# Softplus of a 16-state scan as one ScalarE function in place of a composition

## The chip, the cores and the metric

The kernel runs on one core of a Trainium2 chip. The metric is the device time of one execution in microseconds (us); lower is better. Everything is in 32-bit floating point.

## The reference, cut to what matters

The whole computation is a two-layer network on four images of 128 channels and 64x64 pixels. Layer 0 reorders the pixels of each image by a score, runs a selective scan with 16 states over the 4096 reordered pixels, and puts the result back. Layer 1 runs a scan with 256 states and then a long convolution. The change lies in layer 0's scan:

```python
xc = silu(conv1d(xm) + conv1d_b)                   # 256 channels, 4096 tokens
dbc = xc @ x_proj_w.T                              # 8 + 16 + 16 columns
dt_low, Bc, Cc = dbc[..., :8], dbc[..., 8:24], dbc[..., 24:]
dt = softplus(dt_low @ dt_proj_w.T + dt_proj_b)    # dt_proj_b is -4.6
dA = exp(dt[..., None] * A)                        # A = -exp(A_log), 16 states
dBx = dt[..., None] * Bc[:, :, None, :] * xc[..., None]
h = dA_t * h + dBx_t                               # one step of the scan
y = einsum('bds,bs->bd', h, C_t) + D * xc
y = y * silu(z)
```

So softplus, log(1 + exp(x)), is taken once for every channel and token, 4 x 256 x 4096 values in all.

## The kernel before, in words

The program runs in three parts: a front (layer 0 up to the reordered pixels), `layer0_scan`, and layer 1. The order of the instructions on each engine in `layer0_scan` is written out by hand: engines work through their own list in that order and wait for each other by semaphores.

*Units and steps.* `layer0_scan` cuts each image's 4096 tokens into 8 units of 512 tokens (`PJ`), 32 units in all. A unit has 16 steps: two halves of 256 tokens (`SUB`), times 8 pairs of states. The 256 channels are two halves (`k`) of 128 partitions. Each step works on 128 x 1024 values: two states, two halves of channels, 256 tokens.

*One step.* Every engine has a part in it:

- `fetch` (SP) broadcasts the rows of Bc and Cc for two states to all partitions, five steps ahead, into `bcb` (six buffers).
- `spread` (POOL, L549) multiplies `dx` by the Bc rows into `v` (four buffers), three steps ahead. A small second instruction (L554) adds the state carried over from the half before; `carry` (L544) prepares this from `af`.
- `lift` (ScalarE, L563) computes the factors exp(dt * A) with four Exp activations of 128 x 255 into one of two PSUM buffers `factors`, one step ahead.
- `scan` (VectorE) runs the recurrence (L571) into `states`, then the product with the Cc rows (L575) and a small copy (L576).
- `add_up` (TensorE, L587) sums the products over the states in PSUM; at the end of each half `gated` (VectorE, L603) multiplies the sum by silu(z) into `yg`.

*Beside the steps.* The generator `project` prepares the inputs of the next unit while the present one is scanned. `beside`, called once a step, takes pieces from it. Each `yield` names the kind of the piece that follows: "free" pieces are issued one per step; "mm" and "post" pieces are a matmul into the single PSUM buffer `mm` and what empties it in the next step. `project` yields, in order: two convolutions by four matmuls each (L410, emptied by L415 into `xz`), two matmuls for z (L419, L421), Silu in place on `xz` (L423), the projection to Bc, Cc and dt_low (L427, L430), two matmuls for dt (L439), softplus, the product `dx` of dt and xc (L458, POOL), and `af`, the factors of each half's first token (L463). For unit 0 the whole of `project` is issued before the first step, and unit 1's begins directly behind it.

*Softplus.* It is composed as relu(x) + log(1 + e) + (e - ((1 + e) - 1)), with e = exp(-|x|); the last term gives back what rounding 1 + e loses. Abs (L441) and Relu (L442) read the matmul's PSUM buffer, Exp (L444) runs in place, and Identity with a bias of one (L447), Ln (L449) and Identity with a bias of minus one (L450) follow in one piece; then come three POOL instructions (L452, L454, L456), one to a piece. All but Abs and Relu are 128 x 1024.

*Other side work.* `output` multiplies `yg` by the output weights (L479, copied out by ScalarE at L483) and, once for each of the first three images, `put_back` returns the pixels to their places (L499, VectorE at L505, with `xs` loaded from DRAM). They share the buffer `mm` with `project`, which goes first.

*Tables.* ScalarE's functions come from tables, of which one set is active at a time; the compiler puts a table load (ACT_TABLE_LOAD) before an activation whose function is not in the active set.

The main loop sets the order within a step:

```python
    for j in range(-9, steps):
        if 0 <= j + 5 < steps:
            bcs[j + 5] = fetch(j + 5)
        ...
            vs[j + 3] = spread(j + 3, bcs[j + 3])
        if 0 <= j + 1 < steps:
            lift(j + 1)
        ...
        prods[j] = scan(j, vs.pop(j), bcs.pop(j))
        if j:
            add_up(j - 1, prods.pop(j - 1))
        beside(j)
```

Of the kernel before, what the change touches and what calls it, by code (L numbers as in the profile page):

```python
# [8 lines left out]
F32 = mybir.dt.float32  # L9
AF = mybir.ActivationFunctionType  # L10
ALU = mybir.AluOpType
# [322 lines left out]
PJ = 512  # L334
# [3 lines left out]
def layer0_scan(ctx: ExitStack, tc, ident, w, x, xnt, permd, x2, omd, psum, following):  # L338
# [7 lines left out]
    nc = tc.nc  # L346
    ctx.enter_context(tc.manual_schedule())
    cp = ctx.enter_context(tc.tile_pool(name="b_c", bufs=1))
    big = ctx.enter_context(tc.tile_pool(name="b_big", bufs=2))
    sm = ctx.enter_context(tc.tile_pool(name="b_sm", bufs=1))  # L350
# [10 lines left out]
    def halves(name, src):  # L361
        return load(name, [128, 2], src.rearrange("(k p) -> p k", p=128))
# [9 lines left out]
    db = halves("db", w["dt_proj_b"])  # L372
# [6 lines left out]
    nc.vector.tensor_scalar(an, an, -1.0, None, ALU.mult)  # L379
    ow = load("ow", [128, 2, 128], w["out_proj_w"].rearrange("(k p) c -> p k c", p=128))  # L380
    last = cp.tile([128, NS, 2], F32, name="last")
    one, minus = (cp.tile([128, 1], F32, name=name) for name in ("one", "minus"))
    nc.vector.memset(one, 1.0)
    nc.vector.memset(minus, -1.0)
    factors = [pa.tile([128, 2, 2, SUB], F32, name=f"f{i}") for i in range(2)]
    for da in factors:
        nc.vector.memset(da[:, :, :, 0:1], 0.0)  # L387
# [2 lines left out]
    def middle():  # L390
        return ps_.tile([128, 512], F32, tag="mm", name="mm")
# [5 lines left out]
    def project(b, unit, into):  # L397


        xz, dt, dx, af, bcd = into  # L400
        xin = big.tile([128, 3 + PJ], F32, tag="xin", name="xin")
        nc.sync.dma_start(xin, xnt[b][:, bass.ds(PJ * unit, 3 + PJ)])
        yield "free"
        yield "free"
        for k in range(2):
            yield "mm"
            ps = middle()
            for i in range(4):

                nc.tensor.matmul(  # L410
                    ps, taps[:, i, bass.ts(k, 128)], xin[:, bass.ds(i, PJ)], start=i == 0, stop=i == 3
                )
            yield "hold"
            yield "post"
            nc.scalar.activation(xz[:, k, :], ps, AF.Identity, bias=cb[:, k : k + 1])  # L415
        for k in range(2):
            yield "mm"
            ps = middle()
            nc.tensor.matmul(ps, win[:, bass.ts(2 + k, 128)], xin[:, 3:], start=True, stop=True)  # L419
            yield "post"  # L420
            nc.scalar.copy(xz[:, 2 + k, :], ps)  # L421
        yield "free"
        nc.scalar.activation(xz, xz, AF.Silu)  # L423
        yield "mm"
        ps = middle()
        for k in range(2):
            nc.tensor.matmul(ps[:96], xw[:, k, :], xz[:, k, :], start=k == 0, stop=k == 1)  # L427
        yield "post"
        bc = big.tile([96, PJ], F32, tag="bc", name="bc")
        nc.scalar.copy(bc, ps[:96])  # L430
        nc.sync.dma_start(bcd[0], bc[32 : 32 + NS, :])
        nc.sync.dma_start(bcd[1], bc[64 : 64 + NS, :])


        e = sm.tile([128, 2, PJ], F32, tag="e", name="e")
        for k in range(2):
            yield "mm"
            ps = middle()
            nc.tensor.matmul(ps, dw[:, bass.ts(k, 128)], bc[0:8, :], start=True, stop=True)  # L439
            yield "post"  # L440
            nc.scalar.activation(e[:, k, :], ps, AF.Abs, bias=db[:, k : k + 1])  # L441
            nc.scalar.activation(dt[:, k, :], ps, AF.Relu, bias=db[:, k : k + 1])  # L442
        yield "free"
        nc.scalar.activation(e, e, AF.Exp, scale=-1.0)  # L444
        yield "free"
        e1 = sm.tile([128, 2, PJ], F32, tag="e1", name="e1")
        nc.scalar.activation(e1, e, AF.Identity, bias=one)  # L447
        ln = sm.tile([128, 2, PJ], F32, tag="ln", name="ln")
        nc.scalar.activation(ln, e1, AF.Ln)  # L449
        nc.scalar.activation(e1, e1, AF.Identity, bias=minus)  # L450
        yield "free"
        nc.gpsimd.tensor_tensor(e, e, e1, ALU.subtract)  # L452
        yield "free"
        nc.gpsimd.tensor_tensor(dt, dt, ln, ALU.add)  # L454
        yield "free"
        nc.gpsimd.tensor_tensor(dt, dt, e, ALU.add)  # L456
        yield "free"
        nc.gpsimd.tensor_tensor(dx, dt, xz[:, 0:2, :], ALU.mult)  # L458
        yield "free"
        yield "free"  # L460
        for i in range(PJ // SUB):
            for k in range(2):
                nc.scalar.activation(  # L463
                    af[:, i, :, k], an[:, k, :], AF.Exp, scale=dt[:, k, SUB * i : SUB * i + 1]
                )
# [153 lines left out]
    for _ in project(*units[0], ready[0]):  # L619
        pass  # L620
# [3 lines left out]
    def beside(j):  # L624
        nonlocal rear, holder
        if holder:
            keep = holder.kind == "hold"
            holder.next()
            holder = holder if keep else None
        if ahead[0] < len(units) and j >= per * (ahead[0] - 1) - 9:  # L630
            ready[ahead[0]] = tiles()
            fronts.append(Work(project(*units[ahead[0]], ready[ahead[0]])))
            ahead[0] += 1
        if j == steps - 64:
            extra.append(Work(following))
        while fronts and fronts[0].kind is None:
            fronts.pop(0)
        if (rear is None or rear.kind is None) and behind:
            rear = Work(behind.pop(0))
        for work in (*fronts, rear, *extra):  # L640
            if work and work.kind == "free":
                work.next()
        for work in (*fronts, rear, *extra):
            if work and work.kind == "mm" and holder is None:
                work.next()
                holder = work
# [768 lines left out]
@with_exitstack  # L1415
def conv_attn_hybrid(ctx: ExitStack, tc, w, out):
    nc = tc.nc
    const = ctx.enter_context(tc.tile_pool(name="const", bufs=1))
    dram = ctx.enter_context(tc.tile_pool(name="dram", bufs=1, space=DRAM))
    ident = const.tile([128, 128], F32, name="ident")  # L1420
    make_identity(nc, ident)
    half = const.tile([128, 32], F32, name="half")
    nc.vector.memset(half, -0.5)
    x2 = dram.tile([NB, 128, L], F32, name="x2")
    x3 = dram.tile([NB, 128, L], F32, name="x3")
    x = w["x"]
    xnt = dram.tile([NB, 128, 3 + L], F32, name="xnt")
    pqd = dram.tile([NK, 2, 128, 4, 128], F32, name="pqd")
    mud = dram.tile([128, 4, 3, 128], F32, name="mud")
    permd = dram.tile([128, NB, 2, 256], F32, name="permd")  # L1430
    omd = dram.tile([2, 128, 16, 128], F32, name="omd")
    layer0_front(tc, ident, half, w, x, xnt, permd, pqd, mud)
    pool = ctx.enter_context(tc.tile_pool(name="weights", bufs=1))
    weights = layer1_weights(nc, pool, *(w[k] for k in ("W_in", "W_delta", "W_B", "W_C", "W_out", "A")))
    psum, second = [], []
    work = projection(ctx, tc, ident, half, weights, x2, psum, second)
    first = work[-2](0)
    layer0_scan(tc, ident, w, x, xnt, permd, x2, omd, psum, work[-1](0, 0, first))
    layer1(tc, ident, weights, work, psum, second, w["phi"], pqd, mud, x, omd, permd, first, x2, x3, out)
# [48 lines left out]
```

## Time and profile before

| what | value |
|---|---|
| median of 3 runs | 21374.23 us |
| lowest and highest run | 21372.89 and 21374.53 us |
| profiled execution, first to last instruction | 21377.5 us |
| scan of layer 0, start of first to start of last scan instruction | 626.4 to 2735.4 us |
| VectorE busy, whole span | 20559.4 us (96%) |
| POOL busy, whole span | 20113.6 us (94%) |
| ScalarE busy, whole span | 16041.0 us (75%) |
| TensorE busy, whole span | 17653.8 us (83%) |

The profile comes from one execution, and its span is 3.3 us longer than the median of the runs. In its rows the engines are PE (TensorE matmul), PEld (TensorE weight load), DVE (VectorE), ACT (ScalarE), POOL (GpSimd) and SP (which issues the DMAs). L571 is line 571 of the kernel before. A row of the costliest groups has the line, engine and operation, output <- inputs by name, shapes and count, then the busy time in us and the mean of one instruction in ns, then the engine's idle time just before those instructions and what ended most of it. A row of a timeline has the start and the duration in us; x4 joins four like instructions, and a bracket gives the idle time before and what ended it. A row of a wait view has the total in us, the number of waits and the longest.

### The profile page before, as it was taken

What the parts mean: (1) busy time and instruction counts of PE and PEld (TensorE: products, weight loads), DVE (VectorE), ACT (ScalarE), POOL (GpSimd) and SP (SyncE); (2) the same over time, 40 slices, a digit from 0 to 9 for tenths busy, and PEclk for the clock granted to TensorE, in tenths of its full rate; (3) what the DMA queues carried; (4) which work ended last, traced back from release to release, by engine and by line L of the source; (5) the groups of instructions that cost most, each with busy time, mean ns of one, the idle gap of its engine ahead of it and who ended that gap; (6) DMA issues with size and microseconds to landing.
All of it is one profiled execution on the core that took longest, in us unless ns stands there. A gap on an engine that the chain in (4) does not pass through costs nothing.

```text
span 21377.5 us, 294496 instructions
## 1 busy us (share of the span) xinstructions
PE 17653.8 (83%) x99308; PEld 7751.4 (36%) x99308; DVE 20559.4 (96%) x11871; ACT 16041.0 (75%) x29620; POOL 20113.6 (94%) x5685
## 2 busy tenths in 40 slices
PE   7788854555858888877868999599999999999997
PEld 4344421222323333342323344243434434334434
DVE  7788899999999999999999999999999999999996
ACT  3677767777777777777777777787887787788875
POOL 2677789999999999999999999999999999999996
PEclk8999965776979999998979999799999999999999
DMA  1455554555757777766656777577777777777776
GB/s 68 127 140 139 142 161 153 179 175 167 219 172 221 220 225 222 219 211 194 208 183 220 229 236 237 172 235 232 238 232 229 233 234 233 233 233 230 231 231 189
DMA packets 2499932, 4304.08 MB, mean 201 GB/s; under 512 B 803400, under 2 KB 1322864, under 8 KB 2495216
## 3 DMA queue, kind: packets, MB, share of 16 engines
q1 hardware_dynamic: 2498416, 4285.24, 65.6%
q8 instruction: 784, 12.85, 0.2%
q14 instruction: 732, 6.00, 0.1%
HBM read 3660.02 MB, written 624.17 MB: 200 GB/s over the span
## 4 chain that ended last, share of the span: by engine, by line
DVE 51%; PE 12%; POOL 8%; issue 7%; ACT 6%; DMA 2%; SPq 0%; DVEq 0%; POOLq 0%; ACTq 0%
DVE s L1261 50%; POOL v L1238 8%; PE conv L1195 7%; ACT da L1258 5%; PE yp L1278 3%; PE fin L1137 1%; DMA dlb<-delta 1%; DMA strip<-in_phi 1%; DMA yd<-ye 0%; DVE v L1250 0%; ACT ye L1284 0%; PE mm L1052 0%; ACT t L820 0%; PE mm L884 0%; DVE st L805 0%
## 5 line engine op out<-in xcount | busy, mean ns | idle before, releaser
L1238 POOL TENSOR_TENSOR v<-u,dlb 128x2044 f32<-128x2044 f32 (+1 forms) x4096 | 18223.6, 4518 | 66.2 <-DMA dlb<-delta 42.9
L1261 DVE TENSOR_TENSOR_SCAN s<-da,v 128x1024 f32<-128x1024 f32 x8192 | 18008.3, 2286 | 187.8 <-ACT da L1258 132.0
L1258 ACT ACTIVATE da<-dlb,at 128x511 f32<-128x511 f32 x16384 | 11303.8, 690 | 1984.6 <-DVE s L1261 1485.0
L1195 PE MATMUL conv<-strip,tok 128*128 128x512 f32 (+3 forms) x20480 | 8643.5, 549 | 60.4 <-DMA strip<-in_phi 60.1
L1278 PE MATMUL yp<-s,c 128*32 128x256 f32 x65536 | 4948.7, 431 | 2610.8 <-DVE s L1261 1129.6
L1195 PEld LDWEIGHTS conv<-strip,tok 128*128 128x128 f32 x20480 | 3661.2, 191 | 4152.0 <-issue 3704.2
L1278 PEld LDWEIGHTS yp<-s,c 128*32 128x32 f32 x65536 | 1963.6, 120 | 6385.9 <-issue 2055.4
L1242 ACT COPY v<-vf 128x4 f32<-128x4 f32 x4096 | 814.6, 199 | 2121.4 <-DVE s L1261 2105.0
L1137 PE MATMUL fin<-conved,pq 128*128 128x512 f32 (+1 forms) x3968 | 1786.6, 543 | 10.4 <-ACT sum L1158 5.3
L549 POOL TENSOR_TENSOR v<-dx,bcb 128x1024 f32<-128x1024 f32 x512 | 1207.3, 2358 | 437.5 <-DVE states L571 431.5
L571 DVE TENSOR_TENSOR_SCAN states<-f,v 128x1024 f32<-128x1024 f32 x512 | 1175.9, 2297 | 173.8 <-ACT f L563 125.6
L563 ACT ACTIVATE f<-dt,an 128x255 f32<-128x255 f32 x2048 | 973.5, 476 | 399.2 <-DVE states L571 348.4
L1284 ACT COPY ye<-yp 128x512 f32<-128x512 f32 x2048 | 1186.1, 579 | 26.1 <-PE yp L1278 25.4
L1207 ACT COPY conved<-conv 128x512 f32<-128x512 f32 (+1 forms) x1728 | 986.8, 571 | 224.7 <-PE conv L1195 222.7
L587 PE MATMUL y<-p,ident 128*128 128x512 f32 x2048 | 1008.9, 621 | 132.7 <-DVE p L575 129.1
L1137 PEld LDWEIGHTS fin<-conved,pq 128*128 128x128 f32 x3968 | 662.5, 192 | 383.4 <-issue 283.7
L575 DVE TENSOR_TENSOR p<-states,bcb 128x1024 f32<-128x1024 f32 x512 | 627.1, 1225 | 38.6 <-DVE states L571 0.9
L587 PEld LDWEIGHTS y<-p,ident 128*128 128x128 f32 x2048 | 370.8, 196 | 663.4 <-issue 360.1
L479 PE MATMUL mm<-ow,yg 128*32 128x128 f32 x2048 | 281.2, 296 | 106.5 <-ACT om L483 105.3
L479 PEld LDWEIGHTS mm<-ow,yg 128*32 128x32 f32 x2048 | 235.4, 138 | 212.7 <-ACT om L483 128.4
L410 PE MATMUL mm<-xin,taps 128*128 128x512 f32 x512 | 237.8, 608 | 34.3 <-DVE f L387 20.3
L452 POOL TENSOR_TENSOR e<-e,e 128x1024 f32<-128x1024 f32 x32 | 75.1, 2346 | 197.7 <-DMA bcb<-bcd 162.0
(241 smaller groups left out, 5971.7 us busy)
## 6 DMA issues: line engine op xcount, KB each, us to landing
dlb<-delta SPq DMA_DIRECT2D x4096, 512.0 KB, 4.2
strip<-in_phi SPq DMA_DIRECT2D x1536, 448.0 KB, 4.8
yd<-ye SPq DMA_DIRECT2D x2048, 256.0 KB, 4.1
strip<-in_phi SPq DMA_DIRECT2D x1088, 256.0 KB, 4.4
bcb<-bcd SPq DMA_DIRECT2D x1024, 256.0 KB, 4.2
pq<-pqd SPq DMA_DIRECT2D x1472, 64.0 KB, 3.7
yt<-yd SPq DMA_DIRECT2D x4096, 4.0 KB, 3.4
pq<-pqd SPq DMA_DIRECT2D x256, 128.0 KB, 4.0
```

Of the source, the lines that this page charges most:

```text
L549: nc.gpsimd.tensor_tensor(v, ready[n][2][:, :, bass.ts(i, SUB)].unsqueeze(1).broadcast_to((128, 2, 2, SUB)), bc[:, 0].unsqueeze(2).broadca ...
L563: nc.scalar.activation(factors[j % 2][:, a, k, 1:], ready[n][1][:, k, SUB * i + 1 : SUB * i + SUB], AF.Exp, scale=an[:, k, 2 * g + a : 2 * ...
L571: nc.vector.tensor_tensor_scan(states.rearrange(flat), factors[j % 2].rearrange(flat), v.rearrange(flat), 0.0, ALU.mult, ALU.add)
L587: nc.tensor.matmul(t.rearrange("p k t -> p (k t)"), ident, p[:, a].rearrange("p k t -> p (k t)"), start=g == 0 and a == 0, stop=False, ski ...
L1137: nc.tensor.matmul(fin[:, bass.ds(c0, w)], pq[:, n, :], u[:, bass.ds(c0, w)], start=begin and n == 0, stop=end and not partly, skip_group_ ...
L1195: nc.tensor.matmul(ps[:, skip:], tok[:, 1 - r if side else r, j, :], strip[:, bass.ds(c0 - lo, TS - skip)], start=which == 0 and j == js[0 ...
L1207: nc.scalar.copy(u[:, cols], ps[:, cols])
L1238: nc.gpsimd.tensor_tensor(v[:, 0:n, :, 1:], ready[0][:, :, 1:].unsqueeze(1).broadcast_to((128, n, 2, TS - 1)), dl[:, 0:n, 1:].unsqueeze(2) ...
L1258: nc.scalar.activation(da[:, h, 1:], dl[:, d % VD, 1:], AF.Exp, scale=at[:, h, d : d + 1])
L1261: nc.vector.tensor_tensor_scan(s[:, d % GD].rearrange("p h t -> p (h t)"), da.rearrange("p h t -> p (h t)"), v[:, d % VD].rearrange("p h t ...
L1278: nc.tensor.matmul(yp[i // 2][bass.ts(q, 32), i % 2], c[:, h, t], s[:, :, h, t], start=h == 0, stop=h == 1)
L1284: nc.scalar.copy(ye, yp[j].rearrange("p i d t -> p i t d"))
```

## The change

Softplus is taken by ScalarE's function of that name. The matmul's PSUM buffer is emptied into `dt` by one Identity activation per half with the bias, and one Softplus activation of 128 x 1024 follows in place. Abs, Relu, Exp, the two Identity activations with constants, Ln and the three POOL instructions go, with their tiles `e`, `e1` and `ln`, the constants `one` and `minus` and four of the pauses (`yield "free"`) between the pieces.

```diff
-    one, minus = (cp.tile([128, 1], F32, name=name) for name in ("one", "minus"))
-    nc.vector.memset(one, 1.0)
-    nc.vector.memset(minus, -1.0)
...
-        e = sm.tile([128, 2, PJ], F32, tag="e", name="e")
         for k in range(2):
             yield "mm"
             ps = middle()
             nc.tensor.matmul(ps, dw[:, bass.ts(k, 128)], bc[0:8, :], start=True, stop=True)
             yield "post"
-            nc.scalar.activation(e[:, k, :], ps, AF.Abs, bias=db[:, k : k + 1])
-            nc.scalar.activation(dt[:, k, :], ps, AF.Relu, bias=db[:, k : k + 1])
+            nc.scalar.activation(dt[:, k, :], ps, AF.Identity, bias=db[:, k : k + 1])
         yield "free"
-        nc.scalar.activation(e, e, AF.Exp, scale=-1.0)
-        yield "free"
-        e1 = sm.tile([128, 2, PJ], F32, tag="e1", name="e1")
-        nc.scalar.activation(e1, e, AF.Identity, bias=one)
-        ln = sm.tile([128, 2, PJ], F32, tag="ln", name="ln")
-        nc.scalar.activation(ln, e1, AF.Ln)
-        nc.scalar.activation(e1, e1, AF.Identity, bias=minus)
-        yield "free"
-        nc.gpsimd.tensor_tensor(e, e, e1, ALU.subtract)
-        yield "free"
-        nc.gpsimd.tensor_tensor(dt, dt, ln, ALU.add)
-        yield "free"
-        nc.gpsimd.tensor_tensor(dt, dt, e, ALU.add)
+        nc.scalar.activation(dt, dt, AF.Softplus)
         yield "free"
         nc.gpsimd.tensor_tensor(dx, dt, xz[:, 0:2, :], ALU.mult)
```

## The prediction

> **What bounds the kernel now.** I began with the costliest groups of the page, to find the stage that the change touches and its engine.
>
> ```profile
> span 21377.5 us, 294496 instructions
> ...
> L549 POOL TENSOR_TENSOR v<-dx,bcb 128x1024 f32<-128x1024 f32 x512 | 1207.3, 2358 | 437.5 <-DVE states L571 431.5
> L571 DVE TENSOR_TENSOR_SCAN states<-f,v 128x1024 f32<-128x1024 f32 x512 | 1175.9, 2297 | 173.8 <-ACT f L563 125.6
> L563 ACT ACTIVATE f<-dt,an 128x255 f32<-128x255 f32 x2048 | 973.5, 476 | 399.2 <-DVE states L571 348.4
> ```
>
> The last columns say who waits. POOL's products waited 431.5 us for VectorE's scans, ScalarE's factors 348.4 us: both are fed by VectorE. In the other direction VectorE waited 125.6 us for ScalarE. By its line's own answer, the scan runs from 626.4 to 2737.7 us: 512 steps in which VectorE spends 2.30 (scan) + 1.23 (product p) + 0.15 (copy) us and, with the gaps, 3.81 us a step. So this stage is bound by VectorE, and only its waits can be won. The wait view of VectorE for 626 to 2740 us lists them (total, times, longest):
>
> ```profile
> DVE states L571 <- ACT f L563: 125.6, 61, 61.0
> DVE yg L603 <- PE y L593: 46.5, 38, 2.2
> DVE xs L505 <- DMA xs<-in_x: 22.8, 6, 7.1
> ```
>
> One of the 61 waits is the start (61.04 us before the first scan). The other 60 are 64.5 us: picked out of VectorE's timeline, 28 are 1.7 us or longer (58.2 us: mostly 2.10 or 1.87, the first 3.75) and 32 are under 0.5 us (6.3 us). To see what makes the long ones I read one unit of 16 steps, first ScalarE's timeline (start, duration), then VectorE's.
>
> ```profile
> 1618.35 2.00 ACT L563 ACTIVATE f<-dt,an 128x255 f32<-128x255 f32 x4
> 1620.41 0.69 ACT L441 ACTIVATE e<-mm,db 128x512 f32<-128x512 f32 x1
> 1621.00 0.68 ACT L442 ACTIVATE dt<-mm,db 128x512 f32<-128x512 f32 x1
> 1621.57 1.05 ACT L444 ACTIVATE e<-e 128x1024 f32<-128x1024 f32 x1
> 1622.51 2.01 ACT L563 ACTIVATE f<-dt,an 128x255 f32<-128x255 f32 x4
> ...
> 1625.15 1.15 ACT L447 ACTIVATE e<-e,one 128x1024 f32<-128x1024 f32 x1
> 1626.32 1.28 ACT L449 ACT_TABLE_LOAD   x1
> 1627.61 1.06 ACT L449 ACTIVATE ln<-e 128x1024 f32<-128x1024 f32 x1
> 1628.70 1.15 ACT L450 ACTIVATE e<-e,minus 128x1024 f32<-128x1024 f32 x1
> 1629.87 1.28 ACT L563 ACT_TABLE_LOAD   x1
> 1631.16 2.00 ACT L563 ACTIVATE f<-dt,an 128x255 f32<-128x255 f32 x4
> ```
>
> ```profile
> 1627.48 2.30 DVE L571 TENSOR_TENSOR_SCAN states<-f,v 128x1024 f32<-128x1024 f32 x1
> ...
> 1633.26 2.30 DVE L571 TENSOR_TENSOR_SCAN states<-f,v 128x1024 f32<-128x1024 f32 x1 [2.10 <-ACT f L563]
> ```
>
> Between two sets of factors ScalarE does 6.6 us of other work (1624.52 to 1631.16). Two factor buffers allow it one set ahead, so the next scan, free at 1631.2, starts 2.1 us late. The short waits come the same way from Silu (table, Silu, table: 4.5 us). In the three units per kernel in which the put-back runs, VectorE waits for the DMA of xs instead (7.1 us at most), and there is no long wait on ScalarE.
>
> **What the Trainium skill says.** "ScalarE: Activation LUTs", section "What ACT_TABLE_LOAD costs": a load is 1283 ns and about 1380 ns of drain come with it; every function runs one element a cycle, and with immediate scale and bias costs 186 ns + 0.833 ns an element, 1039 ns for 1024. The trace agrees on the load (1283 ns) and the rate (Exp 1055, Ln 1057 ns), but shows no drain: Ln starts 0.01 us after its load, the load 0.02 us after the work before it. Section "Table sets: the hidden batching unit": a load is needed at each change of set, and Exp and Ln share one. Here they don't: Ln has a load before it and Exp one after it in each unit. "TensorE: Matmul & The Clock Gate", section "Part 1: The HAM clock gate": half clock after an idle window of about 3.4 us. The trace has both: eight taps matmuls take 5.93 us after a long idle time and 3.70 us when they follow closely.
>
> **The change part by part.** The compiled order of the changed program is the old one on TensorE and SP, waits included, and on VectorE but for the two lost memsets (0.06 us each); only ScalarE's and POOL's change.
>
> 1. *Abs goes, Relu becomes Identity.* 64 Activates of 0.68 us go. One remains per half, and the next factors start 0.57 us earlier.
> 2. *Exp, the two additions of a constant and Ln go; one Softplus comes.* Per unit 1.055 + 1.145 + 1.148 us go, and Softplus takes Ln's place. No Softplus is in the trace. I take 1.06 us, as Exp and Ln; from below 1.04 by the skill's page, from above Silu's rate, (1.911 us for 2048), which gives the same. The loads stay: Softplus has one before it, the factors one after it, 62 in the loop as before. One goes at the start.
> 3. *Three POOL instructions of 2.35 us go per unit* (225.6 us). POOL waits for VectorE's scans, so this is nothing, except at the start. A gain for VectorE through less traffic I put at nothing: its product takes 1224 to 1227 ns whatever POOL does. If POOL were late, its longest wait of some 2.4 us would end first; its load only falls.
> 4. *Four pauses go*, so af and dx come up to four steps earlier. af's 0.9 us fits into the 1.2 us that ScalarE has left in a step with a copy of om (3.81 - 2.01 - 0.58); dx's 2.35 us is twice POOL's 1.1 us of waiting in a step, and the four v buffers, three steps ahead, cover it as they cover four such instructions now.
>
> *ScalarE in a unit.* The factors at 1618.35 move to 1617.78, ending 1619.8. Identity waits for its matmul as Abs did: 1620.41 to 1621.10. Load to 1622.40, Softplus to 1623.48, load to 1624.78, factors to 1626.80. The scan that they feed is due at 1627.48: 0.7 us spare. Then om's copy (0.58) and the next factors to 1629.4, due at 1631.2. The long wait is gone, and nothing replaces it. In the units with the longer matmul wait everything shifts together (Abs at 1686.24, scan at 1693.30): again 0.7. In the first unit of the loop the pattern is tighter: Abs waits for a slow matmul; I get factors at 638.8 for a scan due at 637.7, a wait of 1.1 in place of 3.75. Gain: 58.2 - 1.1 = **57 us**. Late next: VectorE itself, the Silu waits (6.3 us) and yg's wait for TensorE.
>
> *The start* (unit 0 runs bare, and unit 1's matmuls before the first scan):
>
> ```profile
> 607.62 0.91 ACT L463 ACTIVATE af<-an,dt 128x16 f32<-128x16 f32 x4 [5.91 <-POOL dt L456]
> 608.43 0.66 ACT L415 ACTIVATE xz<-mm,cb 128x512 f32<-128x512 f32 x1
> ...
> 626.41 2.30 DVE L571 TENSOR_TENSOR_SCAN states<-f,v 128x1024 f32<-128x1024 f32 x1 [61.04 <-ACT f L563]
> ```
>
> af needs dt, so it waits for POOL, and xz of unit 1 stands behind it on ScalarE, and with it TensorE, Silu and the first factors. After: second Identity to 592.1, load, Softplus to 594.5, load, af to 596.7; unit 1's matmuls, 1.2 us earlier, end at 597.8. So xz starts there instead of 608.43: 10.6 us. The next eight matmuls (6.30 us after 10 us idle) follow after 0.8 us and should take 3.70: 2.6 more. POOL has dx near 597 and the first v well before the scan at 613. Gain **13 us** (10.6 if they stay slow).
>
> *Sum:* 57 + 13 = 70 us, at the profiled span: 21377.5 to 21307.5. The views show no time around the span; it is 3.3 us above the median of the runs, 21374.2, so I forecast **21304 us**. The second layer starts after the last output copy of this stage and its program is the same; the gain is carried to the end.
>
> **The rivals.**
> *TensorE's clock moves yg's wait.* After Silu, yg waits 0.73 us where the xw matmuls are quick (18 times) and about 2.2 where they are slow (12 times: 3.63 against 1.96 us). The unit gets shorter and TensorE loses its 3.92 us idle stretch, so this may fall either way: all slow costs 18 x 1.47 = 26 us (gain 44, 21330 us), all quick gives 18 more (88, 21286). With a slow start of 2.6 us too it ends within the bound, 21333.
> *The wait only moves.* If 1 us of unseen time lies at Softplus (a drain), 0.3 us of wait is left in 28 units: gain 60, 21314. With the page's 1.38 us drain at both loads it is 2.1 us, 58 us in all: 12 to 13 left, 21362, no change. The trace's loads without drain speak against it.
> *Slower: Softplus isn't a one-element-a-cycle function.* Place: the same two loads and Softplus. It decides from about 4.2 us a call, since 1.06 + 0.7 spare + the 2.1 us of the old wait + the start's share is used up. At an eighth of the rate, 7.0 us, the wait is 5.2 us in 28 units, 147 against 58, the start gives 7: 21456 us. Silu, Gelu, Exp and Ln all run at one rate, which speaks against.
> *It doesn't do what it says* if Softplus were expanded into several instructions; the compiled order shows one Activate and one load.
>
> **How the numbers follow.** About 0.2% (43 us) is what a measurement can tell from no change. Forecast, with the clock's play: 0.87, of which 0.02 falls within the bound. The wait moves: 0.08, 0.05 of it within. Slow Softplus: 0.04. Rest 0.01 within. Faster 0.88, within 0.08, slower 0.04. Range 21281 (all quick, and 5 us more) to 21334 (all slow and a slow start).
>
> **What would show it.** Right: Softplus near 1.06 us x32; the idle time of VectorE at L571's line on ScalarE down from 125.6 to about 56 (48 at the start, 6 from Silu, 1); first scan near 613 us; period of a plain unit from 64.4 to 62.3 us; POOL's busy time down 226 us and ScalarE's 152, without use beyond this. Wrong: Softplus over 1.8 us, a gap beside its loads, long waits left on the factors, yg's waits well off 46 us, or a longer second layer.

## The result, and the profile after

| kernel | median of 7 runs, us | lowest to highest |
|---|---|---|
| before | 21374.53 | 21372.89 to 21383.01 |
| changed | 21320.29 | 21311.79 to 21323.59 |

The ratio is 0.9973 with a 95% interval of 0.9962 to 0.9984: 54 us, a quarter of a per cent, faster. The forecast was 21304 us, 70 us faster, with a range of 21281 to 21334 us. The range held; of the 70 us, 54 came. Repeated beside the experiments on another occasion the changed kernel gave 21317.41 against 21375.78 us, 58 us.

The page of the changed kernel (same columns as before; lines have moved up by 17, so L554 is the scan, L546 the factors, L532 POOL's products):

```profile
span 21321.9 us, 294235 instructions
...
L532 POOL TENSOR_TENSOR v<-dx,bcb 128x1024 f32<-128x1024 f32 x512 | 1208.0, 2360 | 631.4 <-DVE states L554 625.3
...
L546 ACT ACTIVATE f<-dt,an 128x255 f32<-128x255 f32 x2048 | 977.7, 478 | 489.6 <-DVE states L554 438.5
L554 DVE TENSOR_TENSOR_SCAN states<-f,v 128x1024 f32<-128x1024 f32 x512 | 1176.0, 2297 | 105.5 <-ACT f L546 53.8
```

VectorE's wait for the factors fell from 125.6 to 53.8 us. The two engines that feed it wait longer for it than before: POOL 625.3 instead of 431.5 us, which is what most of the time of the three lost POOL instructions per unit turned into, and ScalarE 438.5 instead of 348.4 us. VectorE's wait view for 590 to 2690 us (total, times, longest):

```profile
DVE yg L586 <- PE y L576: 56.8, 38, 2.9
DVE states L554 <- ACT f L546: 53.8, 33, 46.2
```

Of the 33 waits one is the start (46.2 us), one is 1.33 us in unit 1, and the other 31 together are 6.2 us: the long ones are gone. yg's wait for TensorE is now the larger of the two; it was 49.4 us over the whole stage.

The same place in a unit as shown before, first ScalarE's timeline, then VectorE's:

```profile
1575.11 2.00 ACT L546 ACTIVATE f<-dt,an 128x255 f32<-128x255 f32 x4
1577.73 0.69 ACT L437 ACTIVATE dt<-mm,db 128x512 f32<-128x512 f32 x1 [0.63 <-PE mm L435]
1578.44 1.28 ACT L439 ACT_TABLE_LOAD   x1
1579.74 1.06 ACT L439 ACTIVATE dt<-dt 128x1024 f32<-128x1024 f32 x1
1580.82 1.28 ACT L546 ACT_TABLE_LOAD   x1
1582.11 2.01 ACT L546 ACTIVATE f<-dt,an 128x255 f32<-128x255 f32 x4
```

```profile
1581.04 2.30 DVE L554 TENSOR_TENSOR_SCAN states<-f,v 128x1024 f32<-128x1024 f32 x1
...
1584.51 0.15 DVE L559 COPY last<-states 128x4 f32<-128x4 f32 x1
1584.80 2.30 DVE L554 TENSOR_TENSOR_SCAN states<-f,v 128x1024 f32<-128x1024 f32 x1
```

The factors end at 1584.12 us and the scan that needs them starts, with no bracket, at 1584.80: 0.68 us to spare. In front of it VectorE leaves 0.14 us after the small copy (1584.66 to 1584.80); a gap of 0.13 to 0.14 us, too short for a bracket, stands before most scans. Softplus's own line:

```profile
L439 ACT ACTIVATE dt<-dt x32: 1058/1059/1062, 589.3 to 2554.6; 128x1024 f32<-128x1024 f32 x32
```

The start, in lines of ScalarE's, TensorE's and VectorE's timelines: af no longer waits for POOL, so xz waits only for its own matmuls and the next eight matmuls follow closely, and the first scan comes at 608.60 us instead of 626.41.

```profile
591.66 0.91 ACT L446 ACTIVATE af<-an,dt 128x16 f32<-128x16 f32 x4
593.19 0.69 ACT L412 ACTIVATE xz<-mm,cb 128x512 f32<-128x512 f32 x1 [0.62 <-PE mm L407]
593.93 3.70 PE L407 MATMUL mm<-xin,taps 128*128 128x512 f32 x8 [0.78 <-ACT xz L412]
...
608.60 2.30 DVE L554 TENSOR_TENSOR_SCAN states<-f,v 128x1024 f32<-128x1024 f32 x1 [46.25 <-ACT f L546]
```

### The profile page after: what moved, and what is told of

Its sections match the earlier page's. It is cut to its first block, busy times and chain, and to the rows that moved or that the text cites. A ratio compares the mean times of both kernels' runs of the same rounds, so it can differ in the third digit from the quotient of the medians.

```text
span 21321.9 us, 294235 instructions
## 1 busy us (share of the span) xinstructions
PE 17626.2 (83%) x99308; PEld 7730.6 (36%) x99308; DVE 20560.0 (96%) x11869; ACT 15938.4 (75%) x29459; POOL 19902.7 (93%) x5589
## 4 chain that ended last, share of the span: by engine, by line
DVE 51%; PE 13%; POOL 8%; issue 7%; ACT 6%; DMA 2%; SPq 0%; DVEq 0%; POOLq 0%; ACTq 0%
DVE s L1244 50%; POOL v L1221 7%; PE conv L1178 7%; ACT da L1241 5%; PE yp L1261 3%; PE fin L1120 1%; DMA strip<-in_phi 1%; DMA dlb<-delta 0%; DMA yd<-ye 0%; DVE v L1233 0%; ACT ye L1267 0%; ACT t L803 0%; PE mm L867 0%; DVE st L788 0%; PE mm L1035 0%
## 5 line engine op out<-in xcount | busy, mean ns | idle before, releaser
L532 POOL TENSOR_TENSOR v<-dx,bcb 128x1024 f32<-128x1024 f32 x512 | 1208.0, 2360 | 631.4 <-DVE states L554 625.3
L546 ACT ACTIVATE f<-dt,an 128x255 f32<-128x255 f32 x2048 | 977.7, 478 | 489.6 <-DVE states L554 438.5
L554 DVE TENSOR_TENSOR_SCAN states<-f,v 128x1024 f32<-128x1024 f32 x512 | 1176.0, 2297 | 105.5 <-ACT f L546 53.8
L558 DVE TENSOR_TENSOR p<-states,bcb 128x1024 f32<-128x1024 f32 x512 | 627.0, 1225 | 38.3 <-DVE states L554 0.4
L441 POOL TENSOR_TENSOR dx<-dt,xz 128x1024 f32<-128x1024 f32 x32 | 75.2, 2351 | 155.0 <-ACT dt L439 155.0
```

The source lines that it names most:

```text
L532: nc.gpsimd.tensor_tensor(v, ready[n][2][:, :, bass.ts(i, SUB)].unsqueeze(1).broadcast_to((128, 2, 2, SUB)), bc[:, 0].unsqueeze(2).broadca ...
L546: nc.scalar.activation(factors[j % 2][:, a, k, 1:], ready[n][1][:, k, SUB * i + 1 : SUB * i + SUB], AF.Exp, scale=an[:, k, 2 * g + a : 2 * ...
L554: nc.vector.tensor_tensor_scan(states.rearrange(flat), factors[j % 2].rearrange(flat), v.rearrange(flat), 0.0, ALU.mult, ALU.add)
```

## The experiments

The table has, for each trace, the start (from unit 0's first xz activation to the first scan instruction), the stage (from the first scan instruction to the last) and the rest (from there to the end of the span). The last column is the difference of the medians from the kernel before as it ran beside each.

| kernel | start | stage | rest | median against before |
|---|---|---|---|---|
| before | 54.9 | 2109.0 | 18642.1 | |
| changed | 40.4 | 2059.9 | 18653.4 | -54 |
| changed, again | 42.1 | 2058.1 | 18645.0 | -58 |
| block spread | 54.9 | 2058.9 | 18649.8 | -41 |
| Softplus in unit 0 only | 42.1 | 2111.8 | 18651.0 | -6 |
| Softplus in units 1 to 31 | 54.8 | 2060.6 | 18646.9 | -39 |
| POOL's load put back | 42.1 | 2062.1 | 18641.8 | -57 |
| ScalarE's block filled up | 42.2 | 2100.8 | 18640.3 | -11 |
| changed, preparation later | 33.8 | 2009.6 | 18653.3 | -113 |
| before, preparation later | 44.7 | 2131.6 | 18643.6 | +16 |
| changed, preparation later, images early | 32.1 | 1991.6 | 18643.8 | -133 |

**Block spread.** The kernel before with the long piece on ScalarE cut in three:

```diff
         nc.scalar.activation(e1, e, AF.Identity, bias=one)
+        yield "free"
         ln = sm.tile([128, 2, PJ], F32, tag="ln", name="ln")
         nc.scalar.activation(ln, e1, AF.Ln)
+        yield "free"
         nc.scalar.activation(e1, e1, AF.Identity, bias=minus)
```

> The kernel before with two more pauses only: Identity plus one, Ln, and Identity minus one are each issued in a step of their own. No Softplus, the same table loads, the same work on ScalarE and POOL. Theory (the length of ScalarE's block between two sets of factors is what counts, not its work): the block falls from 6.6 to om 0.58 + load 1.28 + Ln 1.06 + load 1.28 = 4.2 us, the long waits of 58 us go but for about 1 us in unit 1, the start is as before; 21374 - 57 = about 21317 us, give or take 10 for TensorE's clock. Rival (the gain is from work taken off ScalarE or POOL, or from Softplus itself): within 10 us of 21374.

Measured: 21335.47 against 21376.78 us, ratio 0.998 (0.9972 to 0.9987). Its ScalarE timeline shows the shortened block between two sets of factors:

```profile
1597.22 1.99 ACT L565 ACTIVATE f<-dt,an 128x255 f32<-128x255 f32 x4
1599.23 0.58 ACT L485 COPY om<-mm 32x512 f32<-32x512 f32 x1
1599.82 1.28 ACT L450 ACT_TABLE_LOAD   x1
1601.12 1.06 ACT L450 ACTIVATE ln<-e 128x1024 f32<-128x1024 f32 x1
1602.19 1.28 ACT L565 ACT_TABLE_LOAD   x1
1603.49 2.01 ACT L565 ACTIVATE f<-dt,an 128x255 f32<-128x255 f32 x4
```

VectorE's wait view for 590 to 2700 us:

```profile
DVE states L573 <- ACT f L565: 68.3, 35, 60.9
```

The longest is the start; the other 34 waits are 7.4 us together, none over 1 us. Without Softplus, and with every instruction of the composition still there, the stage is 2058.9 us long, as with the change (2058.1 and 2059.9). So the gain in the loop comes from the length of an uninterrupted block, not from the amount of work. The medians say the same: 41 us here, 39 us with Softplus in units 1 to 31 (below). The median is 18 us above the expected 21317, which allowed for 10; it moved by 41 us where the stage is 50 us shorter, and that is taken up in the next section.

**The two places apart.** `if (b, unit) == (0, 0):` or its opposite selects Softplus or the composition in `project`.

> Softplus in unit 0 only, the composition in units 1 to 31. Theory: only the start gains, 14 us by the trace of the change (from the first Identity to the first scan 23.2 us, against 37.5 us from the first Abs): 21360 us, with the long waits of 58 us left. Rival (the whole gain is in the loop): 21374.

> The composition in unit 0 only, Softplus in units 1 to 31. Theory: the long waits go (57 us), less some 7 us that yg's waits grew in the trace of the change: 21317 to 21325 us, and the start stays at that of before. Together with the kernel that has Softplus in unit 0 only this should add up to the change within 10 us. Rival (the parts depend on each other, as when an earlier start shifts everything else): the two don't add up.

Measured: 21371.11 us (ratio 0.9997, 0.9989 to 1.0005) and 21337.89 us (0.9982, 0.9974 to 0.9989) against 21376.78. By the traces the parts are clean: Softplus in unit 0 takes 12.8 us off the start and leaves the stage (+2.8), Softplus in the other units leaves the start and takes 48.4 us off the stage. VectorE's waits on the factors, first with Softplus in unit 0 only (590 to 2740 us), then in units 1 to 31 only (590 to 2705 us):

```profile
DVE states L581 <- ACT f L573: 111.9, 61, 48.0
```

```profile
DVE states L581 <- ACT f L573: 68.8, 35, 60.7
```

By the medians they give 6 and 39, 45 us together, against 54 and 58 for the whole: 9 to 13 us apart, so they add up only roughly. Both medians lie above what was expected, by 11 us and, from the upper end of the range, by 13 us. The 6 us of the start alone cannot be told from nothing, as the interval contains 1; that the start gains is shown by the traces only.

**POOL's load put back.** After dx, in the pauses:

```diff
         yield "free"
+        e = sm.tile([128, 2, PJ], F32, tag="e", name="e")
+        nc.gpsimd.tensor_tensor(e, dt, dx, ALU.subtract)
+        yield "free"
+        nc.gpsimd.tensor_tensor(e, e, dt, ALU.add)
+        yield "free"
+        nc.gpsimd.tensor_tensor(e, e, dx, ALU.add)
         yield "free"
```

> The changed kernel with three POOL instructions of 128x1024 per unit put back on a scratch tile, one to a step in the pauses, so that POOL has its 226 us again but nothing waits for them. Theory (POOL's load costs nothing here): the same as the changed kernel, within 5 us. Rival (part of the gain is POOL's): slower by 10 us or more.

Measured: 21318.31 us, against 21317.41 for the changed kernel beside it. POOL's busy time is 20115.4 us, that of before (20113.6), and in its wait view for 600 to 2700 us the wait for the scans shrinks to make room (it is 627.0 us in the changed kernel's second trace):

```profile
POOL v L538 <- DVE states L560: 415.4, 304, 4.5
```

So POOL's load in the loop costs nothing that can be seen.

**ScalarE's block filled up.** Behind Softplus, in the same piece (`one` is set up as in the kernel before; those lines are left out here):

```diff
         nc.scalar.activation(dt, dt, AF.Softplus)
+        for _ in range(2):
+            e = sm.tile([128, 2, PJ], F32, tag="e", name="e")
+            nc.scalar.activation(e, dt, AF.Identity, bias=one)
```

> The changed kernel with two more Identity instructions of 128x1024 (1.15 us each) between Softplus and the next table load, results unused. Theory: with 0.7 us spare the 2.30 us give a wait of 1.6 us in each of 28 units, 45 us, and 2.3 us at the start: about 21367 us. Rival (ScalarE has more room than that, the gain came from elsewhere): within 10 us of the changed kernel.

Measured: 21364.69 us (ratio 0.9994, 0.9986 to 1.0002), 47 us above the changed kernel beside it, its stage 42.7 us longer. In one unit, ScalarE's timeline has the filled block and the late factors, and VectorE's has the scan that waits for them:

```profile
1540.12 1.06 ACT L441 ACTIVATE dt<-dt 128x1024 f32<-128x1024 f32 x1
1541.21 2.33 ACT L444 ACTIVATE e<-dt,one 128x1024 f32<-128x1024 f32 x2
1543.56 1.28 ACT L551 ACT_TABLE_LOAD   x1
1544.86 2.00 ACT L551 ACTIVATE f<-dt,an 128x255 f32<-128x255 f32 x4
```

```profile
1546.95 2.30 DVE L559 TENSOR_TENSOR_SCAN states<-f,v 128x1024 f32<-128x1024 f32 x1 [1.89 <-ACT f L551]
```

The room of about 0.7 us, worked out before the change was run, decides as expected: 2.3 us of other work there bring the long waits back and take away 47 of the 58 us. That the total came so near the expected 45 us is in part luck. The waits over 1 us are 59 us in 32 places, most of them 1.9 us, where 1.6 us in 28 units were expected; against that, yg's waits are 12 us shorter (44.2 against 55.9 us), those for xs 5 us (16.9 against 21.8 us), and the start lost nothing where 2.3 us were expected.

**The preparation begun later.** The largest wait left in the loop, yg's, stands behind Silu: TensorE's matmuls for Bc and Cc wait for Silu, those for dt wait for the copy of bc, and the sums that yg needs stand behind them in TensorE's queue. The edit, in `beside`:

```diff
-        if ahead[0] < len(units) and j >= per * (ahead[0] - 1) - 9:
+        if ahead[0] < len(units) and j >= per * (ahead[0] - 1) - 7:
```

> The changed kernel with the preparation of the next unit begun 7 steps ahead instead of 9 (one constant in beside), so that the matmuls that wait for Silu and for the copy of bc fall behind the matmuls that yg waits for. Theory: yg's waits fall from 57 us to about 12 (those beside the put-back stay), and the first scan comes some 8 us sooner because Silu of unit 1 is then issued behind the first factors: about 21320 - 53 = 21267 us. Rival (the waits of TensorE for ScalarE only move to another place, or the factors become late): 21310 to 21330 us.

Measured: 21262.39 us, ratio to before 0.9947 (0.9934 to 0.9959), 55 us faster than the changed kernel beside it. VectorE's waits:

```profile
DVE states L554 <- ACT f L546: 43.1, 3, 39.9
DVE xs L488 <- DMA xs<-in_x: 20.2, 6, 5.5
...
DVE yg L586 <- PE y L576: 10.1, 8, 2.9
```

yg's waits went from 56 to 10 us, and the short waits behind Silu went too, which was not foreseen: three waits on the factors are left. All 30 groups of matmuls for Bc and Cc in the loop take 1.96 us in this trace, but that alone would leave 0.73 us in each unit, some 22 us in all; so the order of the queue counts too.

**The same edit on the kernel before.**

> The kernel before, with its composed softplus, and only the one constant of beside changed: the next unit's preparation begins 7 steps ahead instead of 9. Theory (Softplus and the later beginning take away two separate waits): yg's waits fall from 49 to about 10 us, the 6 us of short Silu waits go, the first scan comes some 8 us sooner, and the 58 us of long waits on the factors stay: about 21375 - 53 = 21322 us. Rival (one wait takes the place of the other, so that with the long block on ScalarE the later beginning gives little): 21350 us or more.

Measured: 21391.08 against 21374.87 us, ratio 1.0007 (0.9999 to 1.0016): no gain, and in the trace a stage 22.6 us longer. The expectation was wrong and its rival right:

```profile
DVE states L571 <- ACT f L563: 133.1, 36, 50.6
DVE yg L603 <- PE y L593: 55.2, 32, 4.3
```

Outside the start the waits on the factors rose from 64.5 to 82.5 us: most long waits are now 2.5 to 2.8 us instead of 1.9 to 2.1. And yg's waits did not go. In the unit read here they come at the other half: after the long block ScalarE empties the output's matmuls late, and the sums stand behind those on TensorE (a line of VectorE's timeline, one of TensorE's and one of VectorE's):

```profile
1570.20 2.30 DVE L571 TENSOR_TENSOR_SCAN states<-f,v 128x1024 f32<-128x1024 f32 x1 [2.82 <-ACT f L563]
```

```profile
1570.77 3.29 PE L479 MATMUL mm<-ow,yg 128*32 128x128 f32 x16 [4.41 <-ACT om L483]
```

```profile
1582.40 0.69 DVE L603 TENSOR_TENSOR yg<-y,xz 128x512 f32<-128x512 f32 x1 [0.89 <-PE y L593]
```

So the two edits are not independent: of these two kernels, the later beginning pays only in the one with the short block.

**Images early.** The kernel with the later beginning, and in `put_back` two buffers for xs, both loaded a step ahead:

```diff
-        for h in range(2):
-            xs = sm.tile([128, 8, 4, 64], F32, tag="xs", name="xs")
+        images = [sm.tile([128, 8, 4, 64], F32, tag="xs", name="xs", bufs=2) for h in range(2)]
+        for h, xs in enumerate(images):
+            nc.sync.dma_start(xs.rearrange("c py oy x -> c (py oy x)"), x[b][:, bass.ts(h, L // 2)])
+        yield "free"
+        for h, xs in enumerate(images):
             cols = bass.ts(h, L // 2)
-            nc.sync.dma_start(xs.rearrange("c py oy x -> c (py oy x)"), x[b][:, cols])
```

> The changed kernel with the preparation begun 7 steps ahead, and in put_back both halves of the image loaded into two buffers one step before the first is needed. Theory: of VectorE's 20 us of waiting for xs at the three put-backs some 18 go: 21262 - 18 = about 21244 us. Rival (the wait moves to TensorE's matmuls of the put-back or to yg): 21255 us or more.

Measured: 21241.39 against 21374.87 us, ratio 0.9937 (0.9924 to 0.9951). It is the fastest of all, 133 us below the kernel before. The wait for xs fell from 20.2 to 3.2 us:

```profile
DVE xs L490 <- DMA xs<-in_x: 3.2, 2, 2.1
```

## Why the prediction was right, and where its sizes were off

*The bound and the long waits: right, their worth 3 us too high.* The wait that carried the loop's gain was the one named, 58.2 us in 28 places, and 56.9 of it went (1.33 us left in unit 1, forecast 1.1; 0.64 us in the second trace). But each of these waits contains the 0.13 us that VectorE leaves before most scans anyway. All idle time in front of the scans of the stage, short gaps included, fell from 105.3 to 51.9 us, so the term of 57 us was worth 53.4. The room in a plain unit, worked out as 0.7 us, is 0.68 in the trace, and the filled block shows that it is real. The spread block shows that the block's length alone makes the gain of the loop.

*Softplus's cost: right.* It takes 1.059 us where 1.06 was taken, with a load of 1.28 us on each side and 0.02 us between them; no drain is seen there either. The rivals of a slow function and of an unseen drain fall with that. (With a drain of 1.38 us at both loads some 9 us would have been left, not 12 to 13: the start would have lost 2.8 us too.)

*The start: right in size.* The forecast was 13 us: 14.5 and 12.8 us in two traces, with Softplus in unit 0 alone 12.8. xz follows its matmuls and the next eight matmuls took 3.70 us, as foreseen. The eight before them took 5.12 us in the first trace and 6.75 in the second, which is the difference between the two. (The first trace's first scan is 17.8 us earlier; 3.3 of it was there before unit 0's first xz.)

*POOL at nothing: right.* Its load put back cost nothing that was seen. The busy time that went is smaller than forecast: up to the start of layer 1, POOL's fell by 215 us (forecast 226) and ScalarE's by 133 us (forecast 152). For ScalarE the full lengths of the instructions were summed, but they overlap by about 0.1 us in the trace, as at 1621.00 us in the prediction's lines.

*yg's waits at nothing: too good.* The main sum kept them as they were. In the first trace they are 7.4 us longer (56.8 against 49.4; 55.9 in the second trace): the matmuls behind Silu take long 16 times instead of 12, and 1.96 us 14 times instead of 18. This was the first rival's mechanism, in a quarter of its priced size. That these matmuls then ran in part at half clock is shown at the end. With 53.4 us from the scans, 7.4 lost here and 2.5 us less idle time before xs, the stage should be 48.5 us shorter; it is 49.1.

*"The gain is carried to the end": not seen in full.* The traces put the gain in start and stage together at 63.6 and 63.7 us; the medians moved by 54 and 58. The passage to layer 1 does not lose it: from the last scan instruction of this stage to the first of layer 1 it takes 30.4 to 30.9 us in all eleven traces. Layer 1's scans, from the first to the last, take 18436 to 18449 us and what follows them 173 to 179 us. The first trace of the changed kernel has 18446.7 us for these scans, but with Softplus and POOL's load put back they take 18438.5 us, and before 18437.8. So the 11 us by which that trace's rest is longer are not a price of Softplus, and in the second trace of the same kernel only 3 of them came back. Still, every kernel's median lies 2 to 10 us above what its stage and start promise against the one trace of before, also that of the kernel with the composition throughout and a later beginning (promised +12, measured +16). A part comes from that one trace: in all others the time of the profiled execution is 1.7 us above its span, so by an estimate from this it shows an execution of 21379.2 us, 2 to 5 us above the medians of before. Where the other few microseconds are is left open; one trace of before cannot tell.

## What to carry to other kernels

When one engine feeds another through a few buffers, ask how long its queue is busy with other work between two pieces of feed, not how busy it is: here 6.6 us between two sets of factors cost 2.1 us a unit, and two pauses in the order were worth the same in the stage as the Softplus function. Work out the room that is left (here 0.7 us) before adding anything to such a block. And after one wait is gone look again at the others: the constant that gave 55 us with the short block gave nothing with the long one.

## What the runs showed of the hardware

Softplus ran at the rate of Exp and Ln: 1059 ns for 128x1024, where Exp took 1055 and Ln 1057 ns. The trace of before has 211 table loads: one before the first Exp and one at each of the 210 changes between Exp, Ln, Silu, Sigmoid and Gelu. Identity, Copy, Abs and Relu stand behind other functions without a load. In the changed kernel's trace Softplus changes the table like the others, with 32 loads before it and 32 before the next Exp.

TensorE's four matmuls for Bc and Cc took 1.96 us or 2.4 to 3.7 us at the same place of different units, nearly always after the same idle time of 2.48 us. In units 2 to 31, yg waits 0.73 us behind a group of 1.96 us and 1.85 to 2.2 us behind a longer one. Two neighbouring units of the changed kernel:

```profile
1505.02 3.08 PE L424 MATMUL mm<-xz,xw 128*96 128x512 f32 x4 [2.49 <-ACT xz L420]
```

```profile
1568.91 1.96 PE L424 MATMUL mm<-xz,xw 128*96 128x512 f32 x4 [2.48 <-ACT xz L420]
```

The granted clock of TensorE was 0.61 in the first of these stretches and 1.00 in the second: the trace records half clock from 1505.70 us for 3.41 us. The same holds in every unit of the trace of before and of both traces of the changed kernel: a group of 1.96 us has no half clock in it, and every longer group has. In each of these traces the stretches of half clock begin on a grid of 3.413 us. Where long and short groups alternate in the changed kernel, the stretches come 126.3 us apart, which is 37 steps of this grid and two units (62.4 and 63.9 us). This fits the alternation; what sets off a stretch of half clock was not tried.
